# Copying q and k out of PSUM bank by bank, and spreading the making of the sign weights over the attention, in a convolution-attention kernel

## Chip, cores and metric

One Trainium2 chip, one core. The metric is the device time of one execution in microseconds (us), the median.

## The reference, cut to what matters

Eight images of 32x32 pixels and 384 channels pass through two layers. The argument needs the first attention (six heads of 64, with relative positions) and the sign weights of the feed-forward part.

```python
# layer 0, per image: x is group-normed, 1024 tokens of 384 channels
qkv = x.reshape(b, hw, c) @ qkv_w + qkv_b          # q, k, v: 6 heads x 1024 x 64
attn = einsum('bqd,bkd->bqk', q * SCALE, k)
rel_h = einsum('bhwc,hkc->bhwk', r_q, Rh)          # r_q = q as an image
rel_w = einsum('bhwc,wkc->bhwk', r_q, Rw)
attn = softmax(attn + rel_h[..., None] + rel_w[..., None, :])
x = x + einsum('bqk,bkd->bqd', attn, v) @ proj_w + proj_b
# ... (layer 1: causal attention) ...
# feed-forward, first 5 images only: W1 and W2 become signs, group by group
ste = sign(wg - wg.mean())                         # 5 groups of each weight
y = einsum('btc,oc->bto', x, Wb) + b               # then scaled by an absolute maximum, and clipped
```

## The kernel before: the parts touched

Every fp32 value that enters a score is split into a rounded part ("hi", made by ScalarE) and the rest ("lo", made by VectorE from the same PSUM page and the hi part). A page is one 128x1024 tile: 128 channels (two heads) of q or of k, in two PSUM banks. Pages 0 to 2 are q, 3 to 5 are k. There are two such buffers (`s_tile`), and the scores use them too.

Some names: "rel" are matmuls of q with the relative positions, and "far" copies take their results out of PSUM; after a trip through memory they come back as "near", which casts then split like q and k. A key tile is 128 of the 1024 keys. "den" is the matmul for the sum that the softmax divides by, and oT is the output of the attention. "Cold" matmuls are those that run slow after TensorE stood still: the 12 of a page take 5.31 us otherwise, and 7.1 to 8.2 us when cold.

```python
def project_T(w, cols, xT, name):
    ps = pools.s_tile(name)                        # [128, 2, 512], two banks
    # ... 12 matmuls, 6 per bank, the banks alternating ...

def hi_lo(dst, hi, lo, ps, bias):
    nc.scalar.activation(dst[hi], ps[hi], AF.Identity, bias=bias[hi])
    nc.vector.scalar_tensor_tensor(dst[lo], ps[hi], bias[hi], dst[hi].bitcast(F32), ALU.add, ALU.subtract)

def queries_keys(m):
    ps = project_T(wqkv_sb, ts(m, P), xT, f"qk_{b}_{m}")
    for par in range(2):                           # rows 0-63, then rows 64-127
        hi_lo(dst, rows[par], rows[1 - par], ps, bqk[:, m : m + 1])
        # ... for k: two DMAs of the halves, swapped, into ks ...

for m in range(2 * NPAIR):                         # the order of issue in one image
    queries_keys(m)
    if 0 < m <= NPAIR:
        near.append(positions(m - 1))              # "rel": 8 matmuls, 4 far copies each on ACT and DVE
    if m == NPAIR and unfinished:
        unfinished.pop()()                         # result adds of the image before: 8 on DVE, then stores
# ... split (casts of positions), v matmuls, then the attention: 3 pairs x 8 key tiles ...

def residual():
    if pools.fast and b == 0:
        binarize(pools)                            # all sign weights in one block, at key tile 1 of pair 0
    xt = load_x(pools, b)
    # ... add of a bias on GpSimd ...

def add():                                         # the result adds
    for j in range(NJ):
        nc.vector.scalar_tensor_tensor(xt[:, j, :], y[:, j, :], s, xt[:, j, :], ALU.mult, ALU.add)
```

## Time and profile before

| | before |
|---|---|
| time, median of the first 3 runs | 2672.09 us (2670.13 to 2673.42) |
| span of the profiled run | 2663.5 us |
| mean granted TensorE clock | 0.982 |
| TensorE idle in the span | 116.5 us |

For the lines quoted in this document: a timeline line is start, duration, engine, source line, operation, output <- inputs, shapes, number of instructions, and in brackets the idle time before it with what ended it. A group line is source line, engine, operation, number of instructions, then total busy us and mean ns of one, then the idle time before them with what ended most of it. A wait line is engine, tile and source line that waited, who released it, then total us, times, longest us.

### The profile page before, as it was taken

What the parts mean: (1) busy time and instruction counts of PE and PEld (TensorE: products, weight loads), DVE (VectorE), ACT (ScalarE), POOL (GpSimd) and SP (SyncE); (2) the same over time, 40 slices, a digit from 0 to 9 for tenths busy, and PEclk for the clock granted to TensorE, in tenths of its full rate; (3) what the DMA queues carried; (4) which work ended last, traced back from release to release, by engine and by line L of the source; (5) the groups of instructions that cost most, each with busy time, mean ns of one, the idle gap of its engine ahead of it and who ended that gap; (6) DMA issues with size and microseconds to landing.
All of it is one profiled execution on the core that took longest, in us unless ns stands there. A gap on an engine that the chain in (4) does not pass through costs nothing. (4 is left out here: it accounts for less than half of the span.)

```text
span 2663.5 us, 24967 instructions
## 1 busy us (share of the span) xinstructions
PE 2547.0 (96%) x9538; PEld 1526.1 (57%) x9538; DVE 1603.2 (60%) x2311; ACT 1130.0 (42%) x1417; POOL 112.0 (4%) x106
## 2 busy tenths in 40 slices
PE   7989999999999999999999999999999999999998
PEld 3545575555765556755557555576555555555544
DVE  4895456763477644676545776347764386437652
ACT  3631275531556413764127543155641264126411
POOL 1010001000011000010000100001100010001000
PEclk9989999999999999999999999999999999999999
DMA  6521006010142101150110601013200230015000
GB/s 170 172 107 59 36 1 166 1 60 0 36 97 69 37 23 36 32 134 1 60 36 1 166 1 60 0 36 101 66 24 1 75 92 0 24 41 125 1 1 25
DMA packets 148991, 144.70 MB, mean 54 GB/s; under 512 B 107264, under 2 KB 129664, under 8 KB 147328
## 3 DMA queue, kind: packets, MB, share of 16 engines
q1 hardware_dynamic: 142928, 119.36, 16.1%
q0 software_dynamic: 2880, 23.59, 2.5%
q8 instruction: 77, 1.26, 0.2%
q10 hardware_dynamic: 3056, 0.08, 0.1%
q14 instruction: 50, 0.41, 0.1%
HBM read 75.38 MB, written 42.47 MB: 44 GB/s over the span
## 5 line engine op out<-in xcount | busy, mean ns | idle before, releaser
L545 ACT ACTIVATE f_pr<-f_s 128x1024 f32<-128x1024 f32 x384 | 392.1, 1026 | 402.4 <-PE f_s L541 372.5
L554 DVE TENSOR_TENSOR f_sum<-f_sum,f_pr 128x1024 f32<-128x1024 f32 x288 | 343.7, 1222 | 161.6 <-ACT f_pr L545 160.2
L559 PE MATMUL f_av<-f_pr,f_v 128*64 128x512 f32 x1536 | 359.3, 599 | 0.0
L381 PE MATMUL f_qk<-f_gnT,wqkv_sb 128*128 128x512 f32 x576 | 280.7, 638 | 37.2 <-DVE f_k L436 31.4
L541 PE MATMUL f_s<-f_q,f_k 128*128 128x512 f32 x768 | 260.8, 419 | 10.6 <-ACT f_pr L545 10.6
L541 PE MATMUL f_s<-f_r,unit 128*128 128x512 f32 x768 | 241.8, 396 | 0.0
L541 PE MATMUL f_s<-f_q,f_ks 128*128 128x512 f32 x768 | 241.7, 396 | 0.0
L559 PEld LDWEIGHTS f_av<-f_pr,f_v 128*64 128x64 f32 x1536 | 103.2, 137 | 202.8 <-issue 195.0
L381 PEld LDWEIGHTS f_qk<-f_gnT,wqkv_sb 128*128 128x128 f32 x576 | 115.7, 205 | 171.2 <-issue 161.9
L492 DVE TENSOR_TENSOR f_r<-f_near,f_r 32x1024 fp32r<-32x1024 f32 x96 | 187.6, 1954 | 25.6 <-ACT f_r L491 23.0
L715 PE MATMUL f_s<-f_q,f_lnT 128*128 128x512 f32 (+3 forms) x576 | 200.1, 492 | 0.0
L541 PEld LDWEIGHTS f_s<-f_q,f_k 128*128 128x128 f32 x768 | 125.5, 189 | 120.5 <-issue 46.2
L729 PE MATMUL f_av<-f_v,f_pr 128*128 128x385 f32 x576 | 194.5, 487 | 0.0
L541 PEld LDWEIGHTS f_s<-f_q,f_ks 128*128 128x128 f32 x768 | 145.0, 189 | 34.7
L541 PEld LDWEIGHTS f_s<-f_r,unit 128*128 128x128 f32 x768 | 145.0, 189 | 34.3
L729 PEld LDWEIGHTS f_av<-f_v,f_pr 128*128 128x128 f32 x576 | 108.8, 190 | 78.4 <-issue 11.5
L491 ACT CAST f_r<-f_near 32x1024 fp32r<-32x1024 f32 x96 | 146.0, 1521 | 2.3
L715 PEld LDWEIGHTS f_s<-f_q,f_lnT 128*128 128x128 f32 x576 | 101.0, 190 | 71.3 <-issue 47.3
L391 PE MATMUL f_pj<-wproj_sb,f_oT 128*128 128x384 f32 x384 | 128.1, 491 | 9.6 <-DVE f_oT L607 9.6
L694 PE MATMUL f_q<-f_lnT,wqk 128*128 128x512 f32 x288 | 132.7, 617 | 0.0
L391 PE MATMUL f_v<-wqkv_sb,f_gnT 128*128 128x384 f32 x384 | 127.3, 489 | 3.0 <-ACT f_v L497 3.0
L723 ACT ACTIVATE f_pr<-f_s 128x1024 f32<-128x1024 f32 (+3 forms) x64 | 41.6, 650 | 208.7 <-DVE f_s L720 208.7
(159 smaller groups left out, 3244.6 us busy)
## 6 DMA issues: line engine op xcount, KB each, us to landing
f_far<-f_far SPq DMA_DIRECT2D x48, 512.0 KB, 3.0
f_ks<-f_k SPq DMA_DIRECT2D x96, 256.0 KB, 5.1
f_gnT<-in_xT SPq DMA_DIRECT2D x24, 512.0 KB, 4.5
f_near<-f_far SPq DMA_DIRECT2D x96, 128.0 KB, 3.9
f_x<-in_x SPq DMA_DIRECT2D x32, 384.0 KB, 4.6
out_y<-f_x SPq DMA_DIRECT2D x32, 384.0 KB, 3.9
f_w1a<-w1s POOLq DMA_DIRECT2D x5, 1536.0 KB, 7.1
f_w2a<-w2s POOLq DMA_DIRECT2D x5, 1536.0 KB, 6.6
```

The source lines that it names most:

```text
L381: nc.tensor.matmul(ps[:, half, :], w[:, k, cols], xT[:, k, ts(half, 512)], start=(k == 0), stop=(k == NC - 1),)
L391: nc.tensor.matmul(ps[:, :C], xT[:, k, ts(j, P)], w[:, k, cols], start=(k == 0), stop=(k == NC - 1))
L491: nc.scalar.copy(dst[ts(hi, 32)], src)
L492: nc.vector.tensor_tensor(dst[ts(lo, 32)], src, dst[ts(hi, 32)].bitcast(F32), ALU.subtract)
L541: nc.tensor.matmul(sc[:, half, :], keys[:, ts(c, P)], queries[:, ts(half, 512)], start=(i == 0), stop=(i == 2))
L545: nc.scalar.activation(pr, sc.rearrange("p a n -> p (a n)"), AF.Exp)
L554: nc.vector.tensor_tensor(sums[par], prev, prs[par], ALU.add)
L559: nc.tensor.matmul(avs[half][ts(par, HD), :], v[:, c, ts(h, HD)], prs[par][:, ts(half, 512)], start=(c == 0), stop=(c == NJ - 1),)
L694: nc.tensor.matmul(ps, wqk[:, k, ts(m, P)], xT[:, half, k, :], start=(k == 0), stop=(k == NC - 1))
L715: nc.tensor.matmul(sc[:, half, lo:], xT[:, c // 4, k, ts(c % 4, P)], q[:, half, k, lo:], start=(k == 0), stop=(k == NC - 1),)
L723: nc.scalar.activation(pr, sc[:, c * P :], AF.Exp)
L729: nc.tensor.matmul(av[:, : C + 1], prs[c][:, ts(j - c, P)], v[:, c, :], start=(c == 0), stop=(c == j))
```

## The change

Two independent parts. **The copies:** instead of whole rows (hi of rows 0-63, lo, hi of rows 64-127, lo), each page is copied bank by bank: both hi copies of bank 0, both lo operations of bank 0, then the same for bank 1. The intent is that ScalarE works on bank 1 while VectorE works on bank 0. **The signs:** the making of the sign weights becomes a generator, of which one of 18 steps is issued at each key tile of the first image's attention. The intent is that neither the key tiles nor the buffers stand behind one long block. The diff is whole:

```diff
--- before.py
+++ after.py
@@ -241,6 +241,8 @@
                     part[:, times[which], which, g : g + 1], w[:, :, ts(g, n_out // NG)], AX.XY, ALU.add
                 )
             times[which] += 1
+            if which == 1 or w.shape[1] > 1:
+                yield
         nc.vector.tensor_tensor(part[:, 0], part[:, 0], part[:, 1], ALU.add)
         mean = const.tile([P, 2, NG], F32, name="mean_w")
         nc.gpsimd.partition_all_reduce(
@@ -248,6 +250,7 @@
         )
         for which, n in enumerate((FF // NG * C, C // NG * FF)):
             nc.vector.tensor_scalar_mul(mean[:, which], mean[:, which], 1.0 / n)
+        done = 0
         for which, w, dst, n_out in pieces("sign"):
             gs = n_out // NG
             step = min(C // gs, w.shape[1])
@@ -258,6 +261,10 @@
                     above = above[:, : wg.shape[1] * gs].rearrange("p (k o) -> p k o", o=gs)
                     nc.vector.tensor_scalar(above, wg, m, None, ALU.is_gt)
                     nc.vector.scalar_tensor_tensor(wg, wg, m, above, ALU.is_lt, ALU.subtract, reverse1=True)
+                    done += wg.shape[1] * gs
+                    if done > 600:
+                        done = 0
+                        yield
             if NG * gs < n_out:
                 nc.vector.memset(w[:, :, NG * gs :], 0.0)
             nc.sync.dma_start(out=dst.bitcast(F32), in_=w.rearrange("p k o -> p (k o)"))
@@ -431,22 +438,30 @@
 
             q, k, ks, r = ([pools.image(f"{n}_{b}_{par}", F32R) for par in range(2)] for n in ("q", "k", "ks", "r"))
 
-            def hi_lo(dst, hi, lo, ps, bias):
-                nc.scalar.activation(dst[hi], ps[hi], AF.Identity, bias=bias[hi])
-                nc.vector.scalar_tensor_tensor(dst[lo], ps[hi], bias[hi], dst[hi].bitcast(F32), ALU.add, ALU.subtract)
-
             rows = (slice(0, HD), slice(HD, P))
 
             def queries_keys(m):
                 p = m % NPAIR
+                bias = bqk[:, m : m + 1]
                 ps = project_T(wqkv_sb, ts(m, P), xT, f"qk_{b}_{m}")
-                for par in range(2):
-                    hi, lo = rows[par], rows[1 - par]
-                    dst = (q if m < NPAIR else k)[par][:, p, :]
-                    hi_lo(dst, hi, lo, ps, bqk[:, m : m + 1])
-                    if m >= NPAIR:
-                        nc.sync.dma_start(out=ks[par][hi, p, :].bitcast(F32), in_=dst[lo].bitcast(F32))
-                        nc.sync.dma_start(out=ks[par][lo, p, :].bitcast(F32), in_=dst[hi].bitcast(F32))
+                dst = [(q if m < NPAIR else k)[par][:, p, :] for par in range(2)]
+
+                for half in range(2):
+                    t = ts(half, T // 2)
+                    for par in range(2):
+                        hi = rows[par]
+                        nc.scalar.activation(dst[par][hi, t], ps[hi, t], AF.Identity, bias=bias[hi])
+                    for par in range(2):
+                        hi, lo = rows[par], rows[1 - par]
+                        nc.vector.scalar_tensor_tensor(
+                            dst[par][lo, t], ps[hi, t], bias[hi], dst[par][hi, t].bitcast(F32), ALU.add, ALU.subtract
+                        )
+                if m >= NPAIR:
+                    for par in range(2):
+                        for i in range(2):
+                            nc.sync.dma_start(
+                                out=ks[par][rows[i], p, :].bitcast(F32), in_=dst[par][rows[1 - i]].bitcast(F32)
+                            )
 
 
 
@@ -518,8 +533,6 @@
                 multiply_out(pools)
 
             def residual():
-                if pools.fast and b == 0:
-                    binarize(pools)
                 xt = load_x(pools, b)
                 nc.gpsimd.tensor_tensor(xt, xt, pb.unsqueeze(1).to_broadcast([P, NJ, C]), ALU.add)
                 return xt
@@ -606,6 +619,7 @@
                 for half in range(2):
                     nc.vector.tensor_tensor(oT[:, p, ts(half, 512)], avs[half], rb[:, ts(half, 512)], ALU.mult)
 
+            xt, signs = None, binarize(pools) if b == 0 else None
             first = [None, None]
             for p in range(NPAIR):
                 sums = [pools.page(f"sum0_{b}_{p}_{par}") for par in range(2)]
@@ -618,9 +632,11 @@
                     if c == 1:
                         if p > 0:
                             few = set_aside(p - 1, *last)
-                        if p == 0:
+                        if p == 0 and b > 0:
                             xt = residual()
                         avs = [pools.o_tile(f"av0_{b}_{p}_{half}") for half in range(2)]
+                    if b == 0 and (p, c) >= (0, 1) and xt is None and next(signs, True):
+                        xt = residual()
                     if len(pending) == 2:
                         values(p, pending, sums, avs)
                         if later:
```

## The prediction

> **What bounds the kernel now.** I read the page's busy shares first, then the waits of TensorE, then the timelines around the two largest waits.
>
> ```profile
> PE 2547.0 (96%) x9538; PEld 1526.1 (57%) x9538; DVE 1603.2 (60%) x2311; ACT 1130.0 (42%) x1417; POOL 112.0 (4%) x106
> ```
>
> TensorE (PE) is busy 96% of the span, so it sets the end, and the change takes no matmul away. It can only gain where PE stands still (2663.5 - 2547.0 = 116.5 us) or runs its matmuls slowly. The waits of PE (engine, line, who released it: total us, times, longest) name what fills that:
>
> ```profile
> PE f_qk L381 <- DVE f_k L436: 31.4, 8, 3.9
> PE f_pt L293 <- DVE xn L370: 16.5, 18, 1.9
> PE f_den L589 <- ACT f_oT L578: 10.8, 1, 10.8
> PE f_s L541 <- ACT f_pr L545: 10.6, 13, 1.4
> ```
>
> The first is one wait of 3.9 us per image, in the q and k projections; the third is a single wait of 10.8 us in the whole run. The change touches just these two. The second (layer norm) it leaves alone. Small beside them is PE on DVE f_q, 4.6 us in 5 waits, same code as the first.
>
> **The first wait.** A page of q or k (m = 0 to 5) is 128x1024 in PSUM, two banks, and there are two such buffers. The timeline of image 1 (start, duration; in brackets the idle time before and its releaser), first PE, then ScalarE (ACT), then VectorE (DVE):
>
> ```profile
> 423.35 5.31 PE L381 MATMUL f_qk<-f_gnT,wqkv_sb 128*128 128x512 f32 x12
> 432.59 8.24 PE L381 MATMUL f_qk<-f_gnT,wqkv_sb 128*128 128x512 f32 x12 [3.92 <-DVE f_k L436]
> ```
>
> ```profile
> 421.70 1.11 ACT L435 ACTIVATE f_k<-f_qk,bqk 64x1024 fp32r<-64x1024 f32 x1 [2.86 <-PE f_qk L381]
> 428.70 2.24 ACT L435 ACTIVATE f_k<-f_qk,bqk 64x1024 fp32r<-64x1024 f32 x2 [5.89 <-PE f_qk L381]
> 431.16 1.11 ACT L435 ACTIVATE f_k<-f_qk,bqk 64x1024 fp32r<-64x1024 f32 x1 [0.21 <-DVE f_k L436]
> ```
>
> ```profile
> 429.85 3.80 DVE L436 SCALAR_TENSOR_TENSOR f_k<-f_qk,bqk,f_k 64x1024 fp32r<-64x1024 f32 x3 [2.22 <-ACT f_k L435]
> ```
>
> Page 3 is finished at about 421.7 and ACT copies its first 64 rows at once. Its second 64 rows must wait until DVE has read the first 64. By then ACT's queue holds, ahead of them, the first copy of page 4, and that one waits for PE until 428.70 (idle 5.89). I looked up ACT's order in the built program of before: page 4 rows 0-63, page 3 rows 64-127, page 4 rows 64-127. So page 3's last read, the second of the three DVE operations, ends at about 432.4, and only then may page 5 use its buffer: PE stands 3.92 us. The same 3.92 appears in all eight images.
>
> There is a second price. The 12 matmuls after the wait take 8.24 us against 5.31 for the 12 before it. Over the eight images the page after the wait takes 7.08, 8.24, 8.23, 8.18, 8.05, 8.24, 7.09 and 8.06, together 63.2 against 8 x 5.31 = 42.5: 20.7 us more.
>
> **The second wait.** In image 0 the sign weights are made by DVE in one block. Their rooms are image-sized buffers, of which the attention leaves two free; the attention output oT needs one. ACT's copy into oT:
>
> ```profile
> 158.86 1.07 ACT L578 COPY f_oT<-f_av 128x512 f32<-128x512 f32 x2 [12.32 <-DMA w2s<-f_sign]
> ```
>
> It waits until the last sign piece has left for HBM, and PE with it (148.7 to 159.5). The table of stretches (PE, PEld, DVE, ACT, POOL busy; then granted clock, DMA share):
>
> ```profile
> 80.00:217.00 137.00, 123.28 (x508) 70.04 (x509) 117.03 (x159) 59.61 (x58) 7.26 (x3) 0.95 0.34 124
> 148.00:166.00 18.00, 7.24 (x22) 4.16 (x18) 18.00 (x21) 3.73 (x5) 6.67 (x1) 0.62 0.42 164
> ```
>
> DVE is 100% busy there, and the clock mean falls to 0.62. From 159.86 to 166.28 PE does 12 score and 2 value matmuls, 6.4 us for what takes 3.2 us elsewhere (14 at about 0.23). So this hole costs 10.8 + 3.2 = 14 us. As a cross-check, the first scores to the end of the projection's wait take 143 us in image 0 and 121.6 in image 1; 6 us of the difference are the wqk product that only image 0 does, which leaves 15.
>
> [...] ACT's copy of the second rows starts right after DVE's read of the first (24.87, 26.01, 27.32, 28.46: each after the other). [...] slow matmuls follow the waits of 3.92 and 10.8 and none of about 1 us. [...] 64x1024 out of PSUM takes 1.28 on DVE, 64x512 (the far copies) 0.69; ACT 1.11 and 0.58. [...]
>
> **Part one, copies by banks.** Each page now takes 4 ACT copies of 0.58 (2.32 instead of 2.22) and 4 DVE operations of 0.69 (2.76 instead of 2.56). DVE gets 0.2 x 48 = 10 us more in the run, ACT 5, both beside PE. Chain per page: before 1.11 + 1.28 + 1.11 + 1.28 = 4.8 (trace 4.9). Now bank 0 on ACT 1.16, then DVE on bank 0 (1.38) beside ACT on bank 1, then DVE on bank 1 (1.38): 3.9. More than the 0.9 saved counts that no ACT copy waits for DVE any more: the four are ready as soon as the page is, so page 4 can't slip in between. Page 3 should be free about 4 us after its end, while rel (2.3) and page 4 (4.7) keep PE busy for 7.0. Even 2 us of other DVE work leaves no wait. At stake: 31.4 + 20.7 = 52.1, and 4.6 for q. I choose 49 + 3 = 52, since something in one image or another will remain.
>
> After page 5, ACT has casts, v copies and a table load before the first exp: 15.4 us in image 1 (444.44 to 459.84), with 2.3 of copies 17.7. PE has 16 us of v matmuls plus 1.4 for the first score, 17.4. ACT thus stays level with PE; before, it cost PE 1.2 us. I give this no gain.
>
> **Part two, signs in 18 steps.** The operations are the same, 11.2 us of reductions and 26.1 of signs on DVE, but spread over key tiles 1 of pair 0 to 2 of pair 2. A key tile takes PE about 4.7 us; DVE needs 2.4 for the sums and 1.6 to 2.2 for a step. sign_0 is then done around the end of pair 0, so oT can get its room some 5 us (the time its transfer out takes, 5.1) after it is needed, instead of 30 later. PE has four key tiles, about 19 us, before the den matmul needs the buffers that this copy frees. The wait should go. But 117.0 us of DVE work must fit beside some 123 us of PE: 95%. And x of image 0 is loaded only after the 18th step: two more rounds of transfer out (5 to 8), in (6 to 8) and signs, then load 4.6 and GpSimd 6.7, arriving about when the projection wants it. So of 14 us I count 10.
>
> **Sum.** 52 + 10 - 1 for extra instructions beside the Gelu stage = 61: 2672 - 61 = 2611.
>
> **Rivals.** *A: the wait moves.* The casts or the first exp on ACT, or DVE's backlog (far copies 2.7 and result adds 5.9 per image), hold PE where the k wait did. For it: ACT is level with PE after page 5. Against: [...] 3 us of slack stands at page 5. At 3 us an image it costs 24: 2635. *B: DVE becomes the bound in image 0*, or a sign piece arrives late and holds DVE's queue, or x is late. For it: 95%, and only two rooms for three pieces in and out. Part two then gives 0, at worst -8: 2621 to 2629. *C: everything at stake is won*, 52 + 5 + 14 and 4 of the waits on exp: 2597. A transfer that would hide the gain I don't see: DMA works hard while k is copied, but the first scores need only early pieces.
>
> **Range and chances.** 2611, with 2598 (C) to 2626 (B, or a mild A) as 8 in 10. Faster by over 2% means below 2618.6, a saving of 53.5: the k wait with its cold matmuls nearly suffices alone, but needs to go in all eight images. I say 0.76, within 2% 0.23, slower 0.01.
>
> **What would show it.** In the changed trace: the PE wait on DVE f_k gone or under 0.5 us each; page 5 about 5.3 us long in all images; ACT's copies 64x512, four in a row, about 0.58; mean clock above 0.982; no 10 us wait of den in image 0, oT copied by 140, DVE over 90% busy in its attention. Wrong would be: a new PE wait on f_pr or f_r after the v matmuls of every image; DVE idle on a sign load; the projection of image 0 waiting for x; ACT's queue again holding a copy behind a later page.

Two of its statements stand there without their numbers. In the trace of the kernel before, the DMA share was 0.75 (180 GB/s) from 421 to 445 us, where k of image 1 is copied. And over the 4.5 us after a wait of TensorE, the granted clock was 0.50 (images 0 and 6: 0.62) after the waits of 3.92 us, 0.50 after the one of 10.76, and 1.00 after those of 0.82 to 1.45 us at q, the scores, the projection and the feed-forward; after those of 1.56 or 1.57 us at the layer norm it was 0.62 to 0.72.

## More of the kernel before

Beside the lines shown in the prediction, three groups of the kernel before matter later, by form: ScalarE's hi copy of k, VectorE's lo operation of k, and the result adds.

```profile
L435 ACT ACTIVATE f_k<-f_qk,bqk 64x1024 fp32r<-64x1024 f32 x48 | 53.2, 1109 | 132.3 <-PE f_qk L381 119.7 <-DVE f_k L436 12.5
L436 DVE SCALAR_TENSOR_TENSOR f_k<-f_qk,bqk,f_k 64x1024 fp32r<-64x1024 f32 x48 | 60.9, 1282 | 84.9 <-ACT f_k L435 84.5
L872 DVE SCALAR_TENSOR_TENSOR f_x<-f_y,qs,f_x 128x384 f32<-128x384 f32 x40 | 28.0, 760 | 0.3
```

A page takes 2 x 1.109 us on ScalarE and 2 x 1.282 us on VectorE.

## The result and the profile after

| | before | after |
|---|---|---|
| time, median of 4 runs each | 2671.11 us (2664.60 to 2673.42) | 2634.02 us (2631.67 to 2637.86) |
| ratio | | 0.9866 (0.9844 to 0.9889) |
| span of the profiled run | 2663.5 us | 2636.1 us |
| mean granted TensorE clock | 0.982 | 0.992 |

A ratio is the mean time of one kernel's fast runs over the mean of the other's fast runs of the same rounds, so it is not quite the ratio of the two medians. The change gains 1.3%: about 37 us by the medians, 36 by the ratio. That is within 2%. The prediction was 2611 us, 2598 to 2626.

TensorE's share stays at 96%, but its busy time fell by 14.0 us, from 2547.0:

```profile
PE 2533.0 (96%) x9538; PEld 1514.1 (57%) x9538; DVE 1633.0 (62%) x2407; ACT 1156.7 (44%) x1513; POOL 111.2 (4%) x106
```

The waits of TensorE after, those that the change touched:

```profile
PE f_s L554 <- ACT f_pr L558: 14.9, 13, 1.9
PE f_qk L388 <- DVE f_k L456: 10.5, 5, 3.0
...
PE f_v L398 <- ACT f_v L512: 8.3, 8, 1.1
...
PE f_v L398 <- DVE f_far L484: 4.3, 5, 1.5
...
PE f_s L554 <- ACT f_far L483: 2.8, 3, 0.9
PE f_s L554 <- DVE f_k L456: 2.5, 3, 0.8
...
PE f_den L614 <- DVE f_sum L567: 1.2, 1, 1.2
```

Set them beside those of before. The k wait fell from 31.4 to 10.5, the wait of den from 10.8 to 1.2, and that on f_q from 4.6 to 1.5: 33.6 us less. But f_s on f_pr rose from 10.6 to 14.9, f_v on ACT f_v from 3.0 to 8.3, and the three lines on f_far and f_k (4.3 + 2.8 + 2.5) stood in no list before: 19.2 us more. Net 14.4 us of waits, and with the 14.0 us of busy time 28.4, against 27.4 by which the span fell. So the books close: somewhat over half of the waiting that the change removed came back in other waits. The cold matmuls did shrink: the q and k matmuls took 280.7 us before and 264.2 after.

**The tie that I had said would go.** The first q page of image 0, where nothing else runs; first ScalarE, then VectorE:

```profile
24.06 1.38 ACT L453 ACTIVATE f_q<-f_qk,bqk 64x512 fp32r<-64x512 f32 x2 [10.01 <-PE f_qk L388]
27.04 1.38 ACT L453 ACTIVATE f_q<-f_qk,bqk 64x512 fp32r<-64x512 f32 x2 [1.60 <-DVE f_q L456]
```

```profile
25.47 1.53 DVE L456 SCALAR_TENSOR_TENSOR f_q<-f_qk,bqk,f_q 64x512 fp32r<-64x512 f32 x2 [7.26 <-ACT f_q L453]
28.45 1.53 DVE L456 SCALAR_TENSOR_TENSOR f_q<-f_qk,bqk,f_q 64x512 fp32r<-64x512 f32 x2 [1.45 <-ACT f_q L453]
```

ScalarE does bank 0 (24.06 to 25.44) and then idles 1.60 us until VectorE has read bank 0 (27.00). Only then does it touch bank 1. VectorE idles in turn, 1.45 us. The two engines alternate exactly as before, and the page is held from 24.06 to 29.98, 5.9 us; before it was 4.9. The list of waits in the built program says the same: the activation on bank 1 waits for VectorE's second read of bank 0. That list does not say through which tile (the two engines share the PSUM page and the tile that they write to); e3 below settles it.

The groups by form, after (the rows for q have the same means):

```profile
L453 ACT ACTIVATE f_k<-f_qk,bqk 64x512 fp32r<-64x512 f32 x96 | 65.5, 683 | 95.1 <-DVE f_k L456 63.9 <-PE f_qk L388 30.1
L456 DVE SCALAR_TENSOR_TENSOR f_k<-f_qk,bqk,f_k 64x512 fp32r<-64x512 f32 x96 | 72.0, 750 | 40.7 <-ACT f_k L453 38.9
L888 DVE SCALAR_TENSOR_TENSOR f_x<-f_y,qs,f_x 128x384 f32<-128x384 f32 x40 | 33.2, 881 | 0.5
```

A page now costs ScalarE 4 x 0.683 = 2.73 us (before 2.22) and VectorE 4 x 0.750 = 3.00 (before 2.56). Before, ScalarE's idle time ahead of a k copy was mostly put down to PE (119.7 us against 12.5 on VectorE); now most of it is VectorE's own reads, 63.9.

**Why some k wait stayed, and why it differs from image to image.** Image 2, the worst. ScalarE, VectorE, GpSimd and TensorE, in four fences:

```profile
757.61 1.40 ACT L453 ACTIVATE f_k<-f_qk,bqk 64x512 fp32r<-64x512 f32 x2 [1.16 <-PE f_qk L388]
764.21 2.79 ACT L453 ACTIVATE f_k<-f_qk,bqk 64x512 fp32r<-64x512 f32 x4 [5.21 <-DVE f_k L456]
770.74 1.38 ACT L453 ACTIVATE f_k<-f_qk,bqk 64x512 fp32r<-64x512 f32 x2 [3.73 <-DVE f_k L456]
```

```profile
758.41 4.21 DVE L888 SCALAR_TENSOR_TENSOR f_x<-f_y,qs,f_x 128x384 f32<-128x384 f32 x2
762.65 1.53 DVE L456 SCALAR_TENSOR_TENSOR f_k<-f_qk,bqk,f_k 64x512 fp32r<-64x512 f32 x2
```

```profile
756.53 5.14 POOL L884 TENSOR_SCALAR f_y<-f_y,qu,ql 128x384 f32<-128x384 f32 x8 [7.06 <-issue]
```

```profile
759.28 5.31 PE L388 MATMUL f_qk<-f_gnT,wqkv_sb 128*128 128x512 f32 x12
767.60 7.08 PE L388 MATMUL f_qk<-f_gnT,wqkv_sb 128*128 128x512 f32 x12 [3.01 <-DVE f_k L456]
```

VectorE has two result adds ahead of the lo operations of page 3. They take 4.21 us here, where two undisturbed adds take about 1.2 (the shortest single add is 0.605 us, the median 0.612, the longest 3.675), while GpSimd runs its eight clamps of the same image. ScalarE, tied to VectorE's read, stands idle for 5.21 us with page 3's bank 1 waiting to be copied, and TensorE waits 3.01 us for that buffer. The add of 3.675 us began at 758.41, during the clamps (756.53 to 761.67), and ended at 762.09, just after the last of them; the seven adds of this image after it took 0.607 to 0.619 us. In image 1, where the first two adds took 2.11 us, it was the clamps that took longer, 5.81 us instead of 5.14. That the two engines slow each other where they run side by side is my reading of these times; no run tests what does it. Over images 1 to 5 the first adds took 2.11, 4.21, 3.93, 4.14 and 2.03 us, and the wait for page 5 was 0.9, 3.0, 2.7, 3.0 and 0.8 us: it moves with the adds, almost one for one.

**After page 5** of image 1, ScalarE:

```profile
419.36 0.68 ACT L453 ACTIVATE f_k<-f_qk,bqk 64x512 fp32r<-64x512 f32 x1 [0.91 <-PE f_qk L388]
419.94 2.01 ACT L483 COPY f_far<-f_rel 64x512 f32<-64x512 f32 x4
421.98 0.68 ACT L453 ACTIVATE f_k<-f_qk,bqk 64x512 fp32r<-64x512 f32 x1
424.64 1.39 ACT L453 ACTIVATE f_k<-f_qk,bqk 64x512 fp32r<-64x512 f32 x2 [1.99 <-DVE f_k L456]
426.06 6.14 ACT L506 CAST f_r<-f_near 32x1024 fp32r<-32x1024 f32 x4
...
441.47 1.94 ACT L558 ACTIVATE f_pr<-f_s 128x1024 f32<-128x1024 f32 x2
```

Page 5 is copied from 419.36 to 426.03, 6.7 us, with far copies in between and one more idle wait for VectorE. The casts, the v copies and the first exp queue behind it. The first exp starts 22.1 us after ScalarE's first copy of page 5; before it was 19.0 (440.87 to 459.84). TensorE pays for this at the v matmuls and the second score.

**The signs.** The attention of image 0, TensorE's first score with positions to its projection (columns: window, length, then busy time of PE, PEld, DVE, ACT, POOL with counts, granted clock, DMA share, GB/s):

```profile
76.67:204.02 127.35, 122.41 (x509) 68.00 (x507) 116.36 (x160) 59.18 (x58) 8.74 (x4) 1.00 0.39 142
```

This stretch took 137.9 us before. ScalarE copies the first set-aside page into oT at 122.07, and no sign transfer holds it. The clock is 1.00 (0.95 before, in the 137 us that the prediction shows). The stretch gained 10.5 us.

Put together by stage, in us per image from the traces:

| stage | before | after |
|---|---|---|
| first rel product to first score with positions, images 0 to 7 | 51.4, 48.6, 48.5, 48.5, 48.4, 48.5, 49.5, 50.4 | 48.1, 43.9, 47.7, 47.4, 46.0, 43.8, 46.1, 46.1 |
| from there to the projection | 137.9, 116.6, 116.6, 116.7, 116.5, 116.7, 114.6, 114.8 | 127.4, 117.8, 117.9, 117.7, 117.9, 116.8, 115.2, 115.2 |
| projection to the next image's rel, sum of 7 | 1179.0 | 1183.2 |

The first stage, where the copies are, gained 24.7 us. The attention of the other seven images lost 6.0, and the rest 4.2.

### The profile page after: what moved, and what is told of

It reads as the page before. It is cut to its first block, busy times and chain, and to the rows that moved or that the text cites.

```text
span 2636.1 us, 25170 instructions
## 1 busy us (share of the span) xinstructions
PE 2533.0 (96%) x9538; PEld 1514.1 (57%) x9538; DVE 1633.0 (62%) x2407; ACT 1156.7 (44%) x1513; POOL 111.2 (4%) x106
## 5 line engine op out<-in xcount | busy, mean ns | idle before, releaser
L567 DVE TENSOR_TENSOR f_sum<-f_sum,f_pr 128x1024 f32<-128x1024 f32 x288 | 349.1, 1245 | 147.0 <-ACT f_pr L558 145.8
L554 PE MATMUL f_s<-f_q,f_k 128*128 128x512 f32 x768 | 259.1, 419 | 20.1 <-ACT f_pr L558 14.9
L388 PE MATMUL f_qk<-f_gnT,wqkv_sb 128*128 128x512 f32 x576 | 264.2, 603 | 13.2 <-DVE f_k L456 10.5
L507 DVE TENSOR_TENSOR f_r<-f_near,f_r 32x1024 fp32r<-32x1024 f32 x96 | 192.4, 2004 | 29.9 <-ACT f_r L506 27.0
L731 PE MATMUL f_s<-f_q,f_lnT 128*128 128x512 f32 (+3 forms) x576 | 200.1, 491 | 0.0
L388 PEld LDWEIGHTS f_qk<-f_gnT,wqkv_sb 128*128 128x128 f32 x576 | 108.8, 193 | 130.9 <-issue 121.4
L554 PEld LDWEIGHTS f_s<-f_q,f_ks 128*128 128x128 f32 x768 | 145.8, 190 | 35.7
L731 PEld LDWEIGHTS f_s<-f_q,f_lnT 128*128 128x128 f32 x576 | 100.7, 190 | 71.5 <-issue 47.4
L739 ACT ACTIVATE f_pr<-f_s 128x1024 f32<-128x1024 f32 (+3 forms) x64 | 41.7, 651 | 208.7 <-DVE f_s L736 208.7
```

The source lines that it names most:

```text
L388: nc.tensor.matmul(ps[:, half, :], w[:, k, cols], xT[:, k, ts(half, 512)], start=(k == 0), stop=(k == NC - 1),)
L507: nc.vector.tensor_tensor(dst[ts(lo, 32)], src, dst[ts(hi, 32)].bitcast(F32), ALU.subtract)
L554: nc.tensor.matmul(sc[:, half, :], keys[:, ts(c, P)], queries[:, ts(half, 512)], start=(i == 0), stop=(i == 2))
L567: nc.vector.tensor_tensor(sums[par], prev, prs[par], ALU.add)
L731: nc.tensor.matmul(sc[:, half, lo:], xT[:, c // 4, k, ts(c % 4, P)], q[:, half, k, lo:], start=(k == 0), stop=(k == NC - 1),)
L739: nc.scalar.activation(pr, sc[:, c * P :], AF.Exp)
```

## The experiments

My theory (1) was that the tie between ScalarE's bank-1 copy and VectorE's bank-0 read keeps the gain small. The rivals were (2) that the cut itself costs it, because two pieces take longer than one whole copy (on ScalarE 2 x 0.683 us against 1.109), and (3) that the result adds hold VectorE, whatever the copies do. All ten runs were timed against the kernel before in the same rounds. All outputs are right. To compare runs of different rounds I use "saved", which is (1 - ratio) x 2667 us; the kernel before had medians of 2666.82, 2666.88 and 2665.41 us in the three groups of rounds. The given change saves 35.7 in this unit. By the intervals, a saving of one run is uncertain by 3 to 6 us, and a difference of two by 5 to 8.

| run | time, us | ratio (95%) | saved, us |
|---|---|---|---|
| change as given | 2634.02 | 0.9866 (0.9844 to 0.9889) | 35.7 |
| e1 copies only | 2643.81 | 0.9907 (0.9890 to 0.9924) | 24.8 |
| e2 signs only | 2650.52 | 0.9932 (0.9919 to 0.9945) | 18.1 |
| e3 two tiles a page | 2665.33 | 0.9992 (0.9977 to 1.0006) | 2.1 |
| e4 whole copies, ACT, ACT, DVE, DVE | 2599.83 | 0.9744 (0.9729 to 0.9758) | 68.3 |
| e5 pieces, four ACT then four DVE | 2614.16 | 0.9807 (0.9792 to 0.9822) | 51.5 |
| e6 adds issued later | 2629.96 | 0.9855 (0.9837 to 0.9873) | 38.7 |
| e7 whole copies alone | 2611.97 | 0.9801 (0.9781 to 0.9821) | 53.1 |
| e8 e4 with far copies first | 2643.54 | 0.9908 (0.9892 to 0.9924) | 24.5 |
| e9 adds on GpSimd | 2623.32 | 0.9837 (0.9824 to 0.9851) | 43.5 |
| e10 e4 with adds on GpSimd | 2602.45 | 0.9758 (0.9745 to 0.9771) | 64.5 |

### e1 and e2: each part alone

e1 is the kernel before with the change's `queries_keys`; e2 is the kernel before with the change's generator and no new copies.

```diff
 # e1, against the kernel before: the hunk of queries_keys only
-                    hi_lo(dst, hi, lo, ps, bqk[:, m : m + 1])
+                for half in range(2):
+                    t = ts(half, T // 2)
...
 # e2, against the kernel before: the hunks of binarize, residual and attend0_fast only
+                    if b == 0 and (p, c) >= (0, 1) and xt is None and next(signs, True):
+                        xt = residual()
```

> The kernel before with only the copies by banks (512-column pieces, ACT ACT DVE DVE per bank). By the stage times of the changed kernel this part gave about 17 of its 27 us, so about 2655 us. Theory 1 (inside one two-bank PSUM tile ACT's copies of bank 1 still wait for DVE's reads of bank 0, so a page is held 5.9 us): PE still waits on DVE f_k about 10 us in all, as in the changed kernel, and the 10.8 us den wait of image 0 is back. Rival (the two parts disturb each other): less than 12 us or more than 22 us below before.

> The kernel before with only the sign weights in 18 steps. Image 0's attention was 10.5 us shorter in the changed kernel, so about 2660 us, with the 3.92 us wait on DVE f_k back in all eight images (31.4 us) and no den wait. If the parts are independent, its gain and that of the copies alone add up to 27 us within 3.

Measured: e1 saves 24.8 us and e2 18.1. Waits of TensorE in e1 and then in e2:

```profile
PE f_den L597 <- ACT f_oT L586: 10.8, 1, 10.8
...
PE f_qk L381 <- DVE f_k L449: 6.0, 5, 2.9
```

```profile
PE f_qk L388 <- DVE f_k L443: 31.4, 8, 3.9
```

Each part removes its own wait and leaves the other's. In e2 the attention of image 0 takes 127.1 us, as in the change. Both runs gained more than expected. e1's wait on f_k came to 6.0 us instead of about 10, and its gain lies just above the 22 us beyond which I had named the rival that the parts disturb each other. The two savings add to 42.9, where I had expected 27 within 3 and both together gave 35.7. The last difference, 7.2, is not clear of the noise (some 8), so a disturbance is neither shown nor excluded. Part of it may be luck between traces: in e1's one image had slow adds (wait 2.9), in the change's three had (waits 3.0, 2.7, 3.0).

### e3: take the tie away by two one-bank tiles

Each page becomes two tiles of one bank from the pool of four, and the rel products take a two-bank tile instead.

```diff
-                ps = project_T(wqkv_sb, ts(m, P), xT, f"qk_{b}_{m}")
+                pss = [pools.o_tile(f"qk_{b}_{m}_{half}") for half in range(2)]
...
-                        nc.scalar.activation(dst[par][hi, t], ps[hi, t], AF.Identity, bias=bias[hi])
+                        nc.scalar.activation(dst[par][hi, t], pss[half][hi], AF.Identity, bias=bias[hi])
...
+                    both = pools.s_tile(f"rel_{b}_{p}_{par}")
```

> The changed kernel, but each q or k page is two PSUM tiles of one bank each (from the other pool; the rel products take the two-bank tiles instead), so that nothing ties ACT on bank 1 to DVE on bank 0. Theory 1 (the tie between banks of one tile ate the gain): ACT's four copies of a page run in a row, the page is held about 4 us, the PE wait on DVE f_k falls from 10.5 us to under 2, and the time falls 15 to 25 us below the changed kernel, to 2609 to 2619. Theory 2 (DVE's backlog of result adds and the larger number of instructions hold PE): 2629 to 2639, with waits of 2 to 3 us on DVE f_k left in images 2 to 4.

Measured: 2665.33 us, the same as the kernel before. In time this is a miss; the mechanism is visible all the same. ScalarE and VectorE on page 3 of image 1:

```profile
414.57 2.79 ACT L459 ACTIVATE f_k<-f_qk,bqk 64x512 fp32r<-64x512 f32 x4 [2.99 <-PE f_qk L449]
```

```profile
416.74 3.08 DVE L462 SCALAR_TENSOR_TENSOR f_k<-f_qk,bqk,f_k 64x512 fp32r<-64x512 f32 x4
```

The four copies run in a row, and VectorE starts at 416.74 while ScalarE is busy until 417.36: the two engines read different banks at the same time, with correct results, though they still write to the same tiles as in the change. So the tie went through the PSUM page. No k wait for a page is left, and the first stage takes 45.2 to 46.2 us in images 0 to 5. But the feed-forward stage, projection to next rel, grew from 190 to 197.1 to 200.1 us in images 0 to 4, and there TensorE waits longer:

```profile
PE f_pt L300 <- DVE xn L377: 45.9, 33, 3.7
PE f_y L879 <- ACT f_hi L864: 18.8, 6, 3.7
```

These two were 17.5 and 4.0 us in the change. The likely reason, not tested, is that the pages now share their four buffers with the other matmuls of that stage: the first two q pages of image 1 run in one go behind it (390.21 to 400.67), while in the change they are spread over it from 309.01 on. So in its time e3 shows the tie, and not its price. Its other two stages give a hint of the price: the first takes 360.0 us over all images against 369.1 in the change, the attentions 938.7 against 945.7, together 16 us less. It is a hint only, since the far copies changed as well.

### e4 and e5: keep the tile, change the order

If ScalarE's copies of a page all come before VectorE's, none of them has a read of VectorE to wait for. e5 does this with the change's own pieces, e4 with whole rows.

```diff
 # e4, against the change
-                for half in range(2):
-                    t = ts(half, T // 2)
+                for t in (slice(0, T),):
```

```diff
 # e5, against the change: a second loop over the banks, so four ACT copies, then four DVE operations
                         nc.scalar.activation(dst[par][hi, t], ps[hi, t], AF.Identity, bias=bias[hi])
+                for half in range(2):
+                    t = ts(half, T // 2)
                     for par in range(2):
```

> The changed kernel, but the copies are of whole pages again (64x1024) in the order ACT, ACT, DVE, DVE: no instruction more than before the change, and no ACT copy waits for DVE inside a page. Theory 1 (it is ACT's wait for DVE that costs, banks or not): as good as the two-tile kernel within 5 us, 2609 to 2622, though the page is held 4.8 us. If overlapping the two banks matters by itself: 5 us or more behind the two-tile kernel. Theory 2 (DVE's backlog): 2629 to 2639.

> The changed kernel with the same pieces of 512 columns and the same number of instructions, but all four ACT copies of a page before its four DVE operations, so that no ACT copy waits for DVE inside a page. If the tie between ACT and DVE inside one PSUM tile is the cause: 2598 to 2610, near the whole-page kernel (2600), no PE wait on DVE f_k above 1 us. If the extra instructions of the cut in two are what costs: 2620 to 2634.

Measured: e5 2614.16 us, e4 2599.83 us. e5 has the same instructions as the change, in another order, and is 20 us faster by the medians, 15.8 by what the two save. That is the price of ScalarE's wait for VectorE, with what the scheduler rearranged around it, and it is the test that rival 2 alone cannot pass: the cut is in both. Both expectations of e5 were missed: the result lies between their ranges, because each names a part of the cause.

The tie itself is still in e5, turned around. On the first q page of image 0, ScalarE, then VectorE:

```profile
24.68 2.78 ACT L453 ACTIVATE f_q<-f_qk,bqk 64x512 fp32r<-64x512 f32 x4 [10.04 <-PE f_qk L388]
```

```profile
27.49 3.08 DVE L458 SCALAR_TENSOR_TENSOR f_q<-f_qk,bqk,f_q 64x512 fp32r<-64x512 f32 x4 [8.69 <-ACT f_q L453]
```

VectorE starts only when the fourth copy is done, and the page is held from 24.68 to 30.57, 5.9 us, as long as in the change. So on a bare page the time that it is held is not what e5 gained; what it removed is the stop of ScalarE in the middle of a page, with everything that queues behind that stop. "Untied" below means this: no ScalarE copy waits for VectorE.

The trace of e5, ScalarE then VectorE, pages 3 and 5 of image 1:

```profile
407.91 2.80 ACT L453 ACTIVATE f_k<-f_qk,bqk 64x512 fp32r<-64x512 f32 x4 [2.19 <-PE f_qk L388]
...
420.41 2.78 ACT L453 ACTIVATE f_k<-f_qk,bqk 64x512 fp32r<-64x512 f32 x4 [0.33 <-PE f_qk L388]
```

```profile
409.33 2.40 DVE L890 SCALAR_TENSOR_TENSOR f_x<-f_y,qs,f_x 128x384 f32<-128x384 f32 x3
411.74 3.06 DVE L458 SCALAR_TENSOR_TENSOR f_k<-f_qk,bqk,f_k 64x512 fp32r<-64x512 f32 x4
```

VectorE does its adds ahead of page 3 here too, but ScalarE is done with the page by then and waits for nothing of it. The wait for a page on f_k is gone from the list, and the casts of image 1 start 2.8 us after ScalarE's first copy of page 5 instead of 6.7. The stages differ between the change and e5 by 6.8 us in the first, 10.6 in the attentions and 7.2 from projection to rel. So the tie is paid less in the stage of the copies than after it, where ScalarE is late; which copy makes up which part of the last two sums I did not take apart. Of the attentions the traces show this much: in images 1 to 4 of the change TensorE waits 1.82 to 1.86 us for ScalarE's first exps, against 0.80 to 0.83 in e5, and the score matmuls after that wait are cold (granted clock 0.62 over the next 4.5 us; in image 1 a pair of them goes from 0.63 us to 1.05, and in image 1 of e5 it stays at 0.63).

e4 gains another 14.3 us (16.8 by the savings) over e5. It lies below the 2609 to 2622 that I had expected, and e3, to which I had tied it within 5 us, is 65 us behind. So rival 2 is right as well, for its own part: whole copies take 2.24 and 2.59 us a page, the pieces 2.78 and 3.05. In e4 pages 4 and 5 of image 1 come without a gap on TensorE:

```profile
409.10 10.46 PE L388 MATMUL f_qk<-f_gnT,wqkv_sb 128*128 128x512 f32 x24
```

The 24 matmuls take 10.46 us, and the first stage 41.6 or 41.7 us in images 1 to 5. e4 beats the kernel before by 2.6% and the given change by 1.3%; the last two were not timed in the same rounds.

### e6 and e9: take the adds out of VectorE's way

e6 issues the result adds behind page 5 in the program; e9 gives them to GpSimd, which also runs the clamps.

```diff
 # e6, against the change
-                if m == NPAIR and unfinished:
-                    unfinished.pop()()
+            if unfinished:
+                unfinished.pop()()
             split(0, near[0])
```

```diff
 # e9, against the change (and e10, against e4)
-                    nc.vector.scalar_tensor_tensor(xt[:, j, :], y[:, j, :], s, xt[:, j, :], ALU.mult, ALU.add)
+                    nc.gpsimd.tensor_scalar(y[:, j, :], y[:, j, :], s, None, ALU.mult)
+                    nc.gpsimd.tensor_tensor(xt[:, j, :], y[:, j, :], xt[:, j, :], ALU.add)
```

> The changed kernel with the adds of the previous image's result moved behind page 5 of k, out of DVE's way. If DVE's backlog is the main cause of what was not won: PE's wait on DVE f_k falls from 10.5 us to under 3 and the time to about 2615. If the tie inside the tile is: the 3 us waits in images 2 to 4 shrink to 1, some 8 to 12 us are won (2622 to 2630), and ACT's late start after page 5 (first exp 22 us after PE ends the page, against 19 before the change) stays.

> The changed kernel with the previous image's result adds on GpSimd (a multiply and an add there) instead of DVE, since moving them later in the program did not move them in DVE's queue. In three kernels' traces PE's wait for page 5 is 0.7 to 1.0 us where the first two adds take about 2 us on DVE and 2.7 to 3.0 us where they take about 4. If these adds hold DVE: PE's wait on DVE f_k for page 5 falls from 10.5 us to under 3, the time to 2618 to 2628, still 5 us or more behind the kernel with four ACT copies first (2614), because ACT still stops between the banks. If the adds only fill free time: 2630 to 2638.

e6 is inconclusive: 2629.96 us. The scheduler put the adds into VectorE's queue at the same place as before, so the run did not test what it was to test; the wait on f_k came to 7.4 us. e9 does test it: 2623.32 us, and no TensorE wait for a page on f_k in the list. ScalarE's copies of page 3 in image 2 of e9:

```profile
759.12 1.40 ACT L453 ACTIVATE f_k<-f_qk,bqk 64x512 fp32r<-64x512 f32 x2 [1.15 <-PE f_qk L388]
762.11 1.39 ACT L453 ACTIVATE f_k<-f_qk,bqk 64x512 fp32r<-64x512 f32 x2 [1.60 <-DVE f_k L456]
```

The idle time before bank 1 is 1.60 us instead of 5.21; it is the tie alone, as in the bare page of image 0. So the adds (rival 3) cost the change some 8 us by the savings (11 by the medians), the smaller figure just clear of the noise, some 7. With them gone e9 is still 9 us behind e5, which keeps the adds on VectorE and in which ScalarE does not wait: that is the wait without the adds. The time and this gap are as expected for the case that the adds hold VectorE.

### e7: the copies alone, whole and untied

The kernel before, with e4's order of copies and the signs in one block.

```diff
-                    hi_lo(dst, hi, lo, ps, bqk[:, m : m + 1])
+                for t in (slice(0, T),):
+                    for par in range(2):
+                        hi = rows[par]
+                        nc.scalar.activation(dst[par][hi, t], ps[hi, t], AF.Identity, bias=bias[hi])
...
```

> The kernel before with only the order of the whole-page copies changed to ACT, ACT, DVE, DVE; the signs in one block. What the first part of the prediction counted (52 us) measured alone: about 2616, that is the whole-page kernel's 2600 plus the 16 us that the signs gave alone; the den wait of 10.8 us is back.

Measured: 2611.97 us, saved 53.1. My prediction had counted 52 for the copies. The waits of TensorE show what is left:

```profile
PE f_den L596 <- ACT f_oT L585: 10.8, 1, 10.8
...
PE f_qk L381 <- DVE f_q L448: 4.7, 5, 1.0
```

The 52 was there to be had, but by the order of the instructions and not by the cut. e4 less e7 is 15.2 us, which again is what the signs are worth, against 18.1 in e2; the two agree within the noise.

### e8: an attempt to improve on e4

In e4 TensorE still waits 5.4 us on VectorE's far copies. e8 issues the far copies of a pair ahead of the next page's copies.

```diff
             for m in range(2 * NPAIR):
-                queries_keys(m)
                 if 0 < m <= NPAIR:
                     near.append(positions(m - 1))
+                queries_keys(m)
```

> A try for a better version: the whole-page kernel with the far copies of pair p put ahead of the next page's copies, because in images 0, 6 and 7 ACT took them between the two copies of page 5 and PE then waited 1.8 us for them (5.4 us in all, and some cold matmuls). If that order is the cause: those waits go and 5 to 12 us are won, 2588 to 2595. If the early far copies delay the pages instead: 2600 or more.

A miss: 2643.54 us, 44 slower than e4. The far wait is gone, and a larger one has come. The waits of TensorE, then ScalarE ahead of the first exp of image 1:

```profile
PE f_s L553 <- ACT f_pr L557: 39.5, 8, 5.4
```

```profile
440.90 2.99 ACT L505 CAST f_r<-f_near 32x1024 fp32r<-32x1024 f32 x2
443.91 1.28 ACT L557 ACT_TABLE_LOAD   x1
445.20 1.94 ACT L557 ACTIVATE f_pr<-f_s 128x1024 f32<-128x1024 f32 x2
```

With the positions ready earlier, the scheduler put two casts of a later pair ahead of the first exp. The 5.4 us saved at the far copies stand against 39.5 - 9.6 = 29.9 us more at the first scores.

### e10: e4 with the adds on GpSimd

> The whole-page kernel (ACT, ACT, DVE, DVE) with the result adds on GpSimd too. There PE has no wait on DVE f_k left, so theory 1 expects nothing: 2596 to 2603. If DVE's load in this stage still costs: 2585 to 2594.

Measured: 2602.45 us, saved 64.5 against e4's 68.3; the intervals overlap. Where ScalarE does not wait for VectorE, moving the adds wins nothing that shows. With e9 this makes rival 3, as I had put it ("whatever the copies do"), wrong: the adds cost time where ScalarE's copies wait for VectorE. The pair of e9 with pieces and e5's order was not run.

## Why the prediction was wrong

**What bounds the kernel, and the two waits: right.** TensorE sets the end. The inversion on page 3 in ScalarE's queue was the cause of the 31.4 us, and where it and ScalarE's wait are gone (e4, e7) the wait is gone or down to 1.0 us in all, and page 5 takes 5.31 to 5.39 us. e7 saved 53.1 us against my 52 for the copies.

**The step that failed** is, as the prediction put it: "More than the 0.9 saved counts that no ACT copy waits for DVE any more: the four are ready as soon as the page is". Each page's second pair of ScalarE copies does wait, for 1.60 us in a bare page and up to 5.21 beside the adds. The tie goes through the tile, not through the bank: in the change the copy of bank 1 waits for the read of bank 0 (those 1.60 us), and in e3, with a tile for each bank, VectorE reads from 416.74 while ScalarE copies until 417.36. I had read in the trace that ScalarE waited for VectorE's read, had put that down to the shared bank alone, and did not ask what the program itself guards. The same trace could not bear that reading alone: ScalarE's copy and VectorE's read (rows 64 to 127 and 0 to 63, starting at 27.32 and 26.01) took turns, but there they shared the tile as well as the banks. In place of a hold of 3.9 us came 5.9, and e5, with the same 5.9, shows that the loss came less from the hold than from ScalarE's stop. What of page 4 slipped in ahead of page 3 before is now in its right place, which is why some of the gain came at all.

**A second term was mis-sized:** the pieces. I took 0.58 and 0.69 us from the far copies, which are of the same shape but another operation; the change's pieces measured 0.683 and 0.750. The cut costs ScalarE 24.6 us and VectorE 21.5 in the run (by the groups of before and after, q and k together about 106.3 to 130.9 and 122.5 to 144.0), not 5 and 10. That this matters is shown by e5 against e4: 14 to 17 us, none of which I had in the sum.

Put together as estimates, if the signs are worth 15.2 us beside any copies, the savings give the whole correction: the copies whole and untied 53.1 (e7); cut but untied about 36 (e5's 51.5 less the 15.2 for the signs); cut and tied about 20 (35.7 less 15.2), or 24.8 by e1. So of the 52 counted, the cut took about 17 and ScalarE's wait about 16 (11 by e1), each within some 6 to 8.

**The signs: right, and a little low.** I counted 10 of 14. The attention of image 0 gained 10.5, the whole run 15 to 18 (e4 less e7; e2); where the rest of it comes from I have not separated. The copy into oT came at 122, before the 140 that I had named, and the clock in that stretch rose to 1.00. VectorE was busy for 116.36 of 127.35 us, 91%, and did not become the bound: rival B did not happen.

**The rivals.** Rival A, "the wait moves", with 2635, named the result. Its size was near: 19.2 us of new waits, 2.4 an image, where I had taken 3. That its total came within 1 us of the result is partly luck: it counted neither the pieces nor the 10.5 us of k wait that stayed. Its reason I had half: ScalarE is late at v and at the exps. I had written that ScalarE "stays level with PE" after page 5, and counted on copies of 2.3 us; page 5's copies took 6.7.

**Signs I had named.** The mean clock (0.992), the den wait and the copy into oT came as named. The "PE wait on DVE f_k gone or under 0.5 us each" failed: five waits of 0.8 to 3.0 us stayed. "ACT's copies 64x512, four in a row, about 0.58" failed on both counts. "Page 5 about 5.3 us long in all images" held in images 0, 6 and 7 (5.31) and nearly in 1, 4 and 5 (5.39), but it was 7.08 in images 2 and 3. "Wrong would be: a new PE wait on f_pr or f_r after the v matmuls" came in part: the wait on f_pr was not new, but in images 1 to 5 it grew from about 1.2 us to 1.8.

**The nearness of e5.** The kernel that comes nearest to the one that the prediction described, with pieces and no ScalarE wait, is e5, and it measured 2614.16 us. That it came so near to 2611 is partly luck: e5 carries the loss by the cut, which I had not counted, and gained more from the signs than I had counted.

## What to carry to other kernels

Before you cut a copy so that two engines can work on different banks, find out whether the waits that the program will carry are by bank or by tile. If by tile, first try all of one engine's copies before the other's: that order gained more here (e4, 68.3 us saved) than either cut (the change 35.7, e3 2.1), and it needed no extra instructions. Where one engine stops for another in the middle of its work, look at what the second has ahead of it: here ScalarE's idle time before bank 1 of page 3 in image 2 was 5.21 us with the adds on VectorE and 1.60 without them (e9). And do not cost an operation from another operation of the same size: the far copies' 0.58 us stood for pieces that measured 0.683.

## What else the traces showed

- Pieces by bank in one two-bank tile took turns (the change): ScalarE idle 1.60 us and the page held 5.9 us, where I estimate 4.4 from the pieces' own times (1.38 + 2 x 1.53, ScalarE's second pair hidden). With two one-bank tiles (e3) the engines ran side by side (VectorE from 416.74 beside ScalarE until 417.36).
- One cut cost 2 x 683 - 1109 = 257 ns on ScalarE and 2 x 750 - 1282 = 218 ns on VectorE, and the broken-up version lost to the whole one by 14 us (e5 against e4).
- In the change, page 5 took 7.08 us instead of 5.31 after waits of 3.01 and 2.73 us (granted clock 0.62 over the next 4.5 us), and 5.39 after one of 2.96 (1.00). In the attention slow matmuls follow waits of 1.82 to 1.86 us in images 1 to 4 (0.62), but not one of 1.84 in image 5 (1.00). So the length of the wait alone does not decide.
- A single add of VectorE took 3.675 us beside GpSimd's clamps (eight in 5.14 us, 0.65 each), against a median of 0.612.
